# Matmuls of the identity in PE's planned pauses, and a new set of due times, in a four-layer graph attention kernel

## The chip, the cores and the metric

The kernel runs on one core of one Trainium2 chip. A core has five engines with instruction queues of their own: PE (TensorE, matmuls into PSUM), DVE (VectorE), ACT (ScalarE), POOL (GpSimd) and SP (SyncE, which only issues DMAs here). [...] The metric is the device time of one execution in microseconds (us); lower is better.

## What is computed

Sixteen graphs of 1024 nodes with 256 features each share one adjacency matrix (about 0.8% of the entries set, with the diagonal). Four layers follow one another. Each normalises, applies an attention over the neighbours, and adds the result to x:

```python
h = jnp.maximum(_layernorm(x, axis=-1), 0.0)
x = x + _L0_gnn_ref(h, adj, L0_gnn_W, L0_gnn_a)
...
x = x + _L1_gnn_ref(h, adj, L1_gnn_W, L1_gnn_a)
...
x = x + _L2_gnn_ref(h, adj, L2_gnn_W1, L2_gnn_W2, L2_gnn_W3)
...
x = x + _L3_gnn_ref(h, adj, L3_gnn_W, L3_gnn_a)
```

Layers 0 and 3 have four heads of 64 features. Their score for nodes i and j is `leaky_relu(s_src[i] + s_dst[j])`, masked by the adjacency, followed by a softmax over j and a product with the projected values. Layer 1 is the same with one head of 256. Layer 2's score is the product of two projections of h, and it ends in a relu where the others end in an elu. All is float32.

## The kernel before

The program has two paths. `fast` does the work; `general` is taken only when a check of the inputs fails, and is not run here.

`fast` doesn't issue instructions as it goes. It describes each piece of work as a step of a `Plan`: the engine that does it, a planned duration in us (`cost`), a due time, a function that will issue the instructions, the steps it comes after, and the buffers that it takes and gives back (`plan.add`, line 137 on). When all steps are described, `Plan.order` plays them through on paper: whenever an engine is idle, it starts, of the steps that are ready and whose buffers are free, the one with the earliest due time. A step's end is passed on to other engines 0.2 us later (`LATENCY`). The order in which the steps start in this play is the order in which their functions are then called, and so the order of the instructions in each engine's queue. The due times are priorities, not times at which anything is held back. On the chip each engine works through its queue in order and waits at semaphores, whatever the plan thought of the durations.

The due times come from tables. A period is 165.625 us (`PERIOD`). `LATER` shifts each (graph, layer), `AHEAD` and `LEAD` say how much earlier its opening part (`prologue`) is due, `STEP` spreads that part, `WHEN` places the weights and products of layers 1 and 2, and `SLOT` and `SLOT_LATER` place the sparse work. In `SLOT`, `gather` is how much earlier a gather is due than its unit, `load` is about the loading of x, and `again` and `once` about a second loading of x before the closing addition (of layers 3 and 0, line 1606), all in periods.

The work on PE is, with its planned cost:

- The projection of 128 nodes (`projected`, 0.9 us), from a transposed h that a DMA transpose makes (`move`, line 1311: 1.23 us on SP, then 1.6 and 0.9 us until it has landed), between two ACT copies.
- Layer 1 and 2: for each graph and layer eight steps `attend` (line 1854, 3.48 us), each a sum of eight products over 128 source nodes into one of two PSUM banks, `accb`. When it is done, DVE takes a reciprocal of column 256 (line 1871), and ACT divides columns 0 to 255 by it (line 1877 for layer 1, 1879 for layer 2), after which the bank is given back. Layer 2 has scores and queries on PE too (1.72 us each).
- Layers 0 and 3 of most graphs: sparse, in 15 slots of two (graph, layer) each. For 24 units of each slot, four gathers on POOL (`gather`, line 1735, planned at 1.31 us each) bring rows of a table through an indirect DMA into a `vg` tile, DVE weighs them (lines 1752 and 1761), and PE adds them up (line 1779, 0.94 us a unit). A `vg` tile, of which there are three, is free when PE is done with it.
- Layer 0 of the first graph and layer 3 of the last: dense, 64 steps each of 0.47 us (`steps_a`).

Nearly all matmuls are issued by the helper `product` (line 671, so the profile has them under line 674): one call with 128 stationary columns makes two matmuls of 64 columns each. [...] `buf` (line 666) asks for a tile anew each time that a step takes one, in the home that `Plan.homes` has worked out.

Of the kernel before, what the change touches and what calls it, by code (L numbers as in the profile page):

```python
# [21 lines left out]
P = 128  # L22
# [40 lines left out]
EDGED = {member: members for members in SLOTS for member in members}  # L63
BASE = [SLOT_AT[EDGED[b, 0]] if (b, 0) in EDGED else -0.6 for b in range(16)]
SLOT = {
    'span': 0.6715, 'at': 0.002, 'gather': 0.1559, 'begin': 6.8964, 'load': -2.6706, 'close': 0.8376,
    'edges': 30.2125, 'fill': -5.4149, 'weigh': -0.8387, 'attend': 0.309, 'rows': 0.0278, 'again': -1.2003,
    'once': 0.9411, 'pace': 9.064,
}
SLOT_LATER = {  # L70
    ((1, 0), (2, 0)): 0.1347, ((3, 0), (0, 3)): 0.7221, ((4, 0), (5, 0)): 1.2356, ((6, 0), (1, 3)): 0.946,
    ((7, 0), (2, 3)): 0.8656, ((8, 0), (3, 3)): 1.3324, ((9, 0), (4, 3)): 0.7329, ((10, 0), (5, 3)): 0.8829,
    ((11, 0), (6, 3)): 0.574, ((12, 0), (7, 3)): 0.5056, ((13, 0), (8, 3)): 0.8959, ((14, 0), (9, 3)): 0.7223,
    ((15, 0), (10, 3)): 0.6366, ((11, 3), (12, 3)): 0.9472, ((13, 3), (14, 3)): 1.4115,
}

PERIOD, EARLY = 165.625, 0.983  # L80
START = {0: 0.0, 1: 1.0154, 2: 2.027, 3: 3.1446}
LEAD = {0: 1.3047, 1: 0.0738, 2: 0.8011, 3: -0.2537}
STEP = {0: 0.0638, 1: 0.019, 2: 0.0837, 3: 0}
WHEN = {
    (1, 'weights'): ((0.3988, 0.0481), (1.6881, 0.9484)),
    (1, 'attended'): ((-0.0661, 0.0535), (0.5757, 0.1965)),
    (2, 'weights'): ((0.0014, 0.0211), (0.2452, 0.0602)),
    (2, 'attended'): ((0.4029, 0.0849), (0.4921, 0.1455)),
}

LATER = {
    (0, 0): 0.6744, (0, 1): 0.7927, (0, 2): 0.8401, (0, 3): 0.6401, (1, 0): -0.0906, (1, 1): 0.6495,
    (1, 2): 0.7052, (1, 3): -0.2464, (2, 0): 0.3847, (2, 1): 0.9636, (2, 2): 1.6293, (2, 3): 0.9684,
    (3, 0): 0.2871, (3, 1): 1.8347, (3, 2): 0.909, (3, 3): 1.7204, (4, 0): 0.2668, (4, 1): 0.9127,
    (4, 2): 0.5106, (4, 3): 0.7991, (5, 0): 0.4493, (5, 1): 1.167, (5, 2): 1.8896, (5, 3): 1.2478,
    (6, 0): 1.4069, (6, 1): 1.2537, (6, 2): 1.2951, (6, 3): 1.3435, (7, 0): 1.6461, (7, 1): 1.1917,
    (7, 2): 0.9305, (7, 3): 2.4128, (8, 0): 1.1808, (8, 1): 0.8157, (8, 2): 1.1351, (8, 3): 1.4491,
    (9, 0): 0.2849, (9, 1): 0.6946, (9, 2): 1.0782, (9, 3): 0.8714, (10, 0): 0.848, (10, 1): 1.0053,
    (10, 2): 1.2988, (10, 3): 1.4282, (11, 0): -0.0568, (11, 1): 0.5794, (11, 2): 1.0036, (11, 3): 0.5035,
    (12, 0): 1.2348, (12, 1): 0.8426, (12, 2): 0.8101, (12, 3): 0.8823, (13, 0): 0.5907, (13, 1): 0.6373,  # L100
    (13, 2): 1.2291, (13, 3): 2.0887, (14, 0): 1.1378, (14, 1): 0.1377, (14, 2): 0.8184, (14, 3): 3.6396,
    (15, 0): 0.4651, (15, 1): 1.0589, (15, 2): 2.2223, (15, 3): 5.4015,
}
AHEAD = {
    (0, 0): 5.3604, (0, 1): -3.9636, (0, 2): 1.0958, (0, 3): 0.4878, (1, 0): 4.4827, (1, 1): 1.3166,
    (1, 2): 1.1058, (1, 3): -3.1414, (2, 0): 1.5105, (2, 1): 0.7138, (2, 2): 0.588, (2, 3): 0.6503,
    (3, 0): -0.0881, (3, 1): 2.6718, (3, 2): 2.0939, (3, 3): 0.3548, (4, 0): -0.0676, (4, 1): 0.1131,
    (4, 2): -0.1087, (4, 3): -1.4402, (5, 0): 1.0665, (5, 1): -0.4301, (5, 2): 0.6188, (5, 3): 0.6455,
    (6, 0): -0.8488, (6, 1): 0.3608, (6, 2): 3.0352, (6, 3): 0.3675, (7, 0): -0.3494, (7, 1): -0.2156,
    (7, 2): 1.5593, (7, 3): 1.6384, (8, 0): -0.2572, (8, 1): 2.3309, (8, 2): 0.0821, (8, 3): 0.5845,  # L110
    (9, 0): -1.7754, (9, 1): -0.1769, (9, 2): 2.3775, (9, 3): -0.289, (10, 0): 0.5044, (10, 1): 0.0591,
    (10, 2): -0.0652, (10, 3): 0.1443, (11, 0): -4.6604, (11, 1): -0.1943, (11, 2): 0.7395, (11, 3): -0.9007,
    (12, 0): 0.5393, (12, 1): 0.2581, (12, 2): 3.9858, (12, 3): -2.992, (13, 0): 0.2891, (13, 1): -0.1296,
    (13, 2): 0.2842, (13, 3): -0.9502, (14, 0): 0.2928, (14, 1): -0.0225, (14, 2): 0.1627, (14, 3): 8.5761,
    (15, 0): 0.4367, (15, 1): -1.2495, (15, 2): 2.7098, (15, 3): 0.9033,
}


# [3 lines left out]
class Plan:  # L122
# [5 lines left out]

    LATENCY = 0.2
    TURN, PATIENCE = 0.12, 3.0  # L130

    def __init__(self, free, strict):
        self.free, self.steps, self.wide = dict(free), [], set()
# [16 lines left out]
    def order(self):  # L150
# [9 lines left out]
        for k, s in enumerate(steps):  # L160
            if not left[k]:
                ready[s[0]].append((s[2], k))
        events, now, res, last_wide = [], 0.0, [], False
        self.starts, self.turns = {}, []

        def fits(k):
# [8 lines left out]
        while True:  # L175
            again = True
            while again:
                again = False
                for engine, queue in ready.items():
                    if not idle[engine] or not queue:  # L180
                        continue
                    queue.sort()
                    pick = next((q for q in queue if fits(q[1])), None)
                    if pick is None:
                        continue
                    cost = steps[pick[1]][1]
                    if engine == PE:
                        wide = pick[1] in self.wide
                        if wide != last_wide:
                            stay = (  # L190
                                q for q in queue
                                if q[0] < pick[0] + self.PATIENCE and (q[1] in self.wide) == last_wide and fits(q[1])
                            )
                            pick = next(stay, pick)
                        turns = (pick[1] in self.wide) != last_wide
                        cost = steps[pick[1]][1] + self.TURN * turns
                        last_wide ^= turns
                    queue.remove(pick)
                    k = pick[1]
                    self.turns.append((k, True))  # L200
                    for tag in steps[k][5]:
                        free[tag] -= 1
                    for tag in set(steps[k][5]) & set(at):
                        at[tag] += 1
                    idle[engine] = engine == LAND
                    res.append(k)
                    self.starts[k] = now
                    again = True
                    heapq.heappush(events, (now + cost, k, 0))
                    heapq.heappush(events, (now + cost + self.LATENCY, k, 1))  # L210
            if not events:
                break
            now, k, what = heapq.heappop(events)
            if what == 0:
                idle[steps[k][0]] = True
            else:
                self.turns.append((k, False))
                for tag in steps[k][6]:
                    free[tag] += 1
            for b in behind[k]:  # L220
                if (steps[b][0] == steps[k][0]) == (what == 0):
                    left[b] -= 1
                    if not left[b]:
                        ready[steps[b][0]].append((steps[b][2], b))
# [406 lines left out]
def fast(  # L631
# [34 lines left out]
    def buf(tag, shape, dtype=F32, name=None):  # L666
        pool = psum if tag in ("pp", "acc", "accb") else sb
        home = plan.at[plan.now, tag].pop(0)[1]
        return pool.tile(shape, dtype, name=name or tag, tag=f"{tag}_{home}", bufs=1)

    def product(to, stationary, moving, start, stop):

# [1045 lines left out]
    def steps_c(slot):  # L1718
# [8 lines left out]
        for u in range(UNITS):  # L1727
            t, kt = divmod(u, TILES)
            at = slot.at + SLOT["span"] * PERIOD * u / UNITS
            for g in range(NG):  # L1730

                def gather(u=u, g=g):
                    if g == 0:
                        T["vg", u] = buf("vg", [P, NG, slot.width])
                    nc.gpsimd.indirect_dma_start(  # L1735
                        out=T["vg", u][:, g, :],
                        out_offset=None,
                        in_=slot.table[:, :],
                        in_offset=bass.IndirectOffsetOnAxis(ap=edge_of[:, u * NG + g : u * NG + g + 1], axis=0),
                        bounds_check=N - 1,  # L1740
                        oob_is_err=False,
                    )

                s = plan.add(
                    POOL, 1.31, at - SLOT["gather"] * PERIOD, gather, (*slot.stored, *edges_ready) if g == 0 else (s,), take=() if g else ("vg",)
                )
            got = landed(s, at, 0.4 * slot.width)

# [47 lines left out]
    def steps_b(lay, dues):  # L1796
# [53 lines left out]
        for it in range(NT):  # L1850
# [1 line left out]
            at = dues("attended", it)  # L1852

            def attend(it=it, half=half, t=t):
                acc = T["acc", it] = buf("accb", [P, HALF])
                for jt in range(NT):
                    product(
                        acc[:, : F + 1],
# [240 lines left out]
```

## Time and profile before

| | |
|---|---|
| median of three runs | 3209.26 us |
| lowest and highest of them | 3188.41 and 3211.73 us |
| the profiled execution, its own time | 3179.46 us |
| its span, first to last instruction | 3177.7 us |
| mean granted PE clock | 0.941 |
| PE, DVE, ACT, POOL busy | 2703.7, 2321.0, 2113.2, 1757.8 us |
| `attend` of layers 1 and 2 (`accb`) | 8192 matmuls, 1004.1 us busy |
| gathers (line 1735) | 1440, mean 1122 ns |

The profiled execution is one of its own, 30 us below the median of the runs. The busy time of an engine is the union of its instructions' durations. The granted clock says how much of PE's full clock a throttle let through, as a mean over the stretch. A row of idle time or waits names the instruction whose semaphore came last.

### The profile page before, as it was taken

Reading aid. Unit: us, or ns where it says so; the run is one execution under the profiler, and the core shown is the slowest. Engines: PE = TensorE matmul, PEld = TensorE weight load, DVE = VectorE, ACT = ScalarE, POOL = GpSimd, SP = SyncE. Lnnn points to the kernel's source line nnn. Section 1 sums busy time; section 2 is a strip of 40 time slices with the busy share of each in tenths; the row PEclk is TensorE's granted clock in tenths of the full one; section 3 lists DMA queues with packets and bytes.
Section 4 is the critical chain, followed back from the end, with each engine's and each line's share of the span. In section 5 each row is a group of like instructions: output and inputs, shape, how many; then the busy total and the mean of one; then the engine's idle time right before and its main releaser. Section 6 shows DMA issues by size and latency. Waiting matters only on the chain. (4 is left out here: it accounts for less than half of the span.)

```text
span 3177.7 us, 65299 instructions
## 1 busy us (share of the span) xinstructions
PE 2703.7 (85%) x23759; PEld 1400.6 (44%) x23759; DVE 2321.0 (73%) x4581; ACT 2113.2 (67%) x5987; POOL 1757.8 (55%) x1570
## 2 busy tenths in 40 slices
PE   6577889788789899887989898999898899898787
PEld 4342454334446444343444444444444444344335
DVE  8786747777776677767767787878777776776578
ACT  5657695766868657777667767758676657567432
POOL 1046426765652456646656676666656654674570
PEclk9889899898899999999989999999999999999899
DMA  6346455756664467676665767667656654666551
GB/s 188 101 114 172 121 133 153 194 165 183 149 169 96 133 168 184 172 156 188 154 173 150 192 167 176 166 179 173 176 148 165 164 139 130 158 178 151 138 155 32
DMA packets 506519, 492.76 MB, mean 155 GB/s; under 512 B 317380, under 2 KB 428740, under 8 KB 506192
## 3 DMA queue, kind: packets, MB, share of 16 engines
q0 software_dynamic: 115200, 287.05, 33.1%
q1 hardware_dynamic: 390304, 200.67, 26.4%
q8 instruction: 192, 3.15, 0.4%
q14 instruction: 135, 1.11, 0.1%
q10 hardware_dynamic: 688, 0.79, 0.1%
HBM read 460.65 MB, written 65.01 MB: 165 GB/s over the span
## 5 line engine op out<-in xcount | busy, mean ns | idle before, releaser
L1735 POOL DMA_INDIRECT vg<-table,edge_of x1440 | 1615.8, 1122 | 1024.2 <-PE acc L1779 478.1
L674 PE MATMUL accb<-val,p 128*64 128x257 f32 x8192 | 1004.1, 390 | 70.2 <-issue 34.7
L1761 DVE TENSOR_TENSOR vg<-vg,w 128x1040 f32<-128x1040 f32 x720 | 895.0, 1243 | 26.0 <-issue 0.2
L674 PEld LDWEIGHTS accb<-val,p 128*64 128x64 f32 x8192 | 618.9, 140 | 442.3 <-issue 137.6
L1779 PE MATMUL acc<-vg,pick 128*32 128x260 f32 x5760 | 472.9, 405 | 95.3 <-DVE vg L1761 51.4
L674 PE MATMUL pp<-w,hTp 128*64 128x264 f32 (+1 forms) x3072 | 426.9, 412 | 113.5 <-ACT hTp L1325 45.6
L674 PE MATMUL pp<-qT,hT 128*64 128x512 f32 x2048 | 482.0, 604 | 19.4 <-issue 6.8
L674 PEld LDWEIGHTS pp<-w,hTp 128*64 128x64 f32 x3072 | 225.5, 144 | 303.9 <-issue 103.8
L1779 PEld LDWEIGHTS acc<-vg,pick 128*32 128x32 f32 x5760 | 173.7, 112 | 402.1 <-issue 164.5
L1281 ACT ACTIVATE h<-xt,nshift,rstd 128x256 f32<-128x256 f32 x512 | 276.2, 597 | 59.7 <-DVE nshift L1243 41.9
L1307 ACT COPY planes<-h 128x512 uint16<-128x512 uint16 x496 | 281.8, 621 | 20.5 <-DMA turned<-planes 18.3
L1599 ACT ACTIVATE o<-acc,rden 128x64 f32<-128x64 f32 x960 | 219.2, 323 | 101.0 <-DVE rden L1592 66.7
L674 PEld LDWEIGHTS pp<-qT,hT 128*64 128x64 f32 x2048 | 147.6, 138 | 283.7 <-issue 235.1
L1836 ACT ACTIVATE u<-pp 128x512 f32<-128x512 f32 x256 | 154.8, 605 | 152.6 <-PE pp L674 84.8
L1240 POOL TENSOR_TENSOR rstd<-rstd,neg_half 128x8 f32<-128x8 f32 (+2 forms) x67 | 122.6, 1831 | 221.0 <-DVE rstd L1237 186.0
L1325 ACT COPY hTp<-turned 128x1024 uint16<-128x1024 uint16 x184 | 213.4, 1168 | 24.1 <-DMA turned<-planes 20.3
L1380 ACT ACTIVATE vs<-pp,vs 128x64 f32<-128x64 f32 x960 | 223.3, 316 | 0.0
L1193 DVE BATCH_NORM_STATS2 bn<-xt 128x6 f32<-128x256 f32 x512 | 203.2, 421 | 17.9 <-DMA xt<-in_x_dram 4.4
L1841 DVE SCALAR_TENSOR_TENSOR p<-u,p 128x512 f32<-128x512 f32 x256 | 175.3, 685 | 46.0 <-ACT p L1837 34.1
L674 PE MATMUL pp<-w2v,hT 128*64 128x256 f32 x1024 | 154.8, 437 | 63.0 <-ACT hT L1325 45.6
L1564 DVE SCALAR_TENSOR_TENSOR o<-ex,o 128x512 f32<-128x512 f32 (+1 forms) x256 | 142.0, 555 | 69.9 <-ACT ex L1560 58.1
L1842 DVE TENSOR_TENSOR p<-p,mask 128x512 f32<-128x512 f32 x256 | 177.1, 692 | 8.8
(153 smaller groups left out, 2440.7 us busy)
## 6 DMA issues: line engine op xcount, KB each, us to landing
table<-vs SPq DMA_DIRECT2D x120, 264.0 KB
xt<-in_x_dram SPq DMA_DIRECT2D x123, 256.0 KB
vg<-table,edge_of POOLq DMA_INDIRECT x1440
out_dram<-xt SPq DMA_DIRECT2D x64, 256.0 KB
kept<-xt SPq DMA_DIRECT2D x60, 256.0 KB
xt<-kept SPq DMA_DIRECT2D x60, 256.0 KB
raw<-in_adj_dram SPq DMA_DIRECT2D x32, 256.0 KB
row<-er_d SPq DMA_DIRECT2D x32, 256.0 KB
```

The costliest lines, as they stand in the source:

```text
L674: nc.tensor.matmul(to[c : c + COLS], stationary[:, c : c + COLS], moving, start=start, stop=stop, skip_group_check=True,)
L1193: nc.vector.bn_stats(mean_var[b][:, t, :, :].rearrange("p s e -> p (s e)"), of[b, t // 2][:, t % 2, :])
L1281: nc.scalar.activation(h, (x_in if layer == 0 else x_tiles)[b, t // 2][:, t % 2, :], AF.Relu, bias=T["shift"][:, t : t + 1], scale=T["rstd ...
L1307: nc.scalar.copy(to[:, :, :, k, :], of)
L1325: nc.scalar.copy(bits, T["tp", t0].rearrange("p s c q -> p c q s"))
L1380: nc.scalar.mul(to[:, hd, :], of[:, hd, :], a[:, hd, :])
L1599: nc.scalar.mul(to[:, hd, :], of[:, hd, :d], rden[:, hd, :])
L1735: nc.gpsimd.indirect_dma_start(out=T["vg", u][:, g, :], out_offset=None, in_=slot.table[:, :], in_offset=bass.IndirectOffsetOnAxis(ap=edge ...
L1761: nc.vector.tensor_tensor(values, values, w[:, :, m, :].unsqueeze(3).to_broadcast([P, NG, heads, d + 1]), OP.mult)
L1779: nc.tensor.matmul(acc[g * GROUP : (g + 1) * GROUP], pick[:, u, g * GROUP : (g + 1) * GROUP], vg[:, g, lo : lo + heads * (d + 1)], start=k ...
L1841: nc.vector.scalar_tensor_tensor(p, u, 1.0, p, op0=OP.max, op1=OP.mult)
L1842: nc.vector.tensor_mul(p, p, mask_of(half, jt))
```

## The change

Three things are changed.

First, `Plan.order` notes when PE was busy. Whenever PE is idle in the play and no step can start, it adds up PE's planned busy time in the last 3.4 us. If that is under 65% and PE has steps left, it puts in a step of 0.45 us that takes no buffer and comes after nothing, at that place of the order. PE is then taken for 0.45 us in the play too. The step's function, `keep_busy`, issues two products of the identity with itself, 128 columns each, into columns 384 to 511 of the first `accb` bank. Their result is never read.

Second, the two `accb` tiles are made once, before all steps, and `attend` picks one of them by the home that the plan worked out. Before, each `attend` asked for a new tile in that home.

Third, all tables of due times have other values, and the planned cost of a gather is 1.45 us where it was 1.31. The mean of `LATER`'s 64 entries goes from 1.07 to 0.39 periods, that of `SLOT_LATER`'s 15 from 0.84 to 0.18, that of `AHEAD`'s 64 from 0.51 to 0.62.

```diff
 SLOT = {
-    'span': 0.6715, 'at': 0.002, 'gather': 0.1559, 'begin': 6.8964, 'load': -2.6706, 'close': 0.8376,
-    'edges': 30.2125, 'fill': -5.4149, 'weigh': -0.8387, 'attend': 0.309, 'rows': 0.0278, 'again': -1.2003,
-    'once': 0.9411, 'pace': 9.064,
+    'span': 0.6625, 'at': 0.0375, 'gather': 0.0743, 'begin': 6.4905, 'load': -1.9066, 'close': 0.7661,
+    'edges': 31.0052, 'fill': -2.7808, 'weigh': -0.8326, 'attend': 0.4626, 'rows': 0.0277, 'again': 0.9994,
+    'once': 0.595, 'pace': 9.064,
 }
...
-PERIOD, EARLY = 165.625, 0.983
-START = {0: 0.0, 1: 1.0154, 2: 2.027, 3: 3.1446}
-LEAD = {0: 1.3047, 1: 0.0738, 2: 0.8011, 3: -0.2537}
-STEP = {0: 0.0638, 1: 0.019, 2: 0.0837, 3: 0}
+PERIOD, EARLY = 165.625, 1.0283
+START = {0: 0.0, 1: 1.0294, 2: 2.0269, 3: 3.1395}
+LEAD = {0: 1.2991, 1: 0.0803, 2: 1.0096, 3: -0.2434}
+STEP = {0: 0.0519, 1: 0.0021, 2: 0.137, 3: 0.0046}
...
 LATER = {
-    (0, 0): 0.6744, (0, 1): 0.7927, (0, 2): 0.8401, (0, 3): 0.6401, (1, 0): -0.0906, (1, 1): 0.6495,
...
+    (0, 0): -2.2609, (0, 1): 0.3716, (0, 2): -0.1125, (0, 3): -0.5687, (1, 0): -2.2721, (1, 1): -0.4437,
...
     TURN, PATIENCE = 0.12, 3.0
+    SPAN, SHARE, FILL = 3.4, 0.65, 0.45
+    fill = None
...
         events, now, res, last_wide = [], 0.0, [], False
+        stretches, pe_left = [], sum(s[0] == PE for s in steps)
...
                     idle[engine] = engine == LAND
+                    if engine == PE:
+                        stretches.append((now, now + cost))
+                        pe_left -= 1
...
             if not events:
                 break
+            if self.fill and idle[PE] and pe_left:
+                share, n = 0.0, len(stretches) - 1
+                while n >= 0 and stretches[n][1] > now - self.SPAN:
+                    share += stretches[n][1] - max(stretches[n][0], now - self.SPAN)
+                    n -= 1
+                if share < self.SHARE * self.SPAN:
+                    k = len(steps)
+                    steps.append([PE, self.FILL, now, self.fill, (), (), ()])
+                    behind.append([])
+                    stretches.append((now, now + self.FILL))
+                    idle[PE] = False
+                    res.append(k)
+                    self.starts[k] = now
+                    heapq.heappush(events, (now + self.FILL, k, 0))
             now, k, what = heapq.heappop(events)
...
+    banks = [psum.tile([P, HALF], F32, name=f"bank{n}", tag=f"bank{n}", bufs=1) for n in range(bufs["accb"])]
+
+    def keep_busy():
+        for n in range(2):
+            product(banks[0][:, HALF - P :], ident, ident, True, True)
+
+    plan.fill = keep_busy
...
-                    POOL, 1.31, at - SLOT["gather"] * PERIOD, gather, (*slot.stored, *edges_ready) if g == 0 else (s,), take=() if g else ("vg",)
+                    POOL, 1.45, at - SLOT["gather"] * PERIOD, gather, (*slot.stored, *edges_ready) if g == 0 else (s,), take=() if g else ("vg",)
...
-                acc = T["acc", it] = buf("accb", [P, HALF])
+                acc = T["acc", it] = banks[plan.at[plan.now, "accb"].pop(0)[1]]
```

## The prediction

> **What bounds the kernel now.** I read the page first: busy shares, the forty slices with the granted clock, and the chain of waits.
>
> ```profile
> span 3177.7 us, 65299 instructions
> ...
> PE 2703.7 (85%) x23759; PEld 1400.6 (44%) x23759; DVE 2321.0 (73%) x4581; ACT 2113.2 (67%) x5987; POOL 1757.8 (55%) x1570
> ...
> PEclk9889899898899999999989999999999999999899
> ...
> PE 19%; DVE 10%; issue 4%; DMA 3%; ACT 3%; another core or an unknown queue 2%; POOL 1%; POOLq 0%; DVEq 0%; SPq 0%; ACTq 0%
> ```
>
> PE is the fullest engine, but 474 us of the span find it idle. The chain's shares add up to 42%: it was followed back only that far. Of what was followed, PE is 19/42 = 0.45, and DVE 0.24. So I reckon that one us put on PE, or taken off it, moves the end by 0.45 us.
>
> Then the core's clock (mean 0.941) and one place where it fell, cut into windows of 3.41 us; columns are the window's length, busy time of each engine (instructions), clock, DMA share and GB/s.
>
> ```profile
> 1373.57:1376.99 3.42, 3.09 (x32) 1.79 (x31) 2.79 (x6) 3.31 (x10) 2.94 (x4) 1.00 1.17 298
> 1376.99:1380.40 3.41, 0.00 (x0) 0.00 (x0) 3.35 (x10) 0.00 (x0) 2.77 (x4) 1.00 1.24 118
> 1380.40:1383.81 3.41, 0.00 (x0) 0.00 (x0) 1.84 (x5) 0.41 (x1) 2.92 (x3) 0.50 1.10 119
> 1383.81:1387.23 3.42, 1.60 (x8) 1.00 (x10) 2.29 (x2) 1.76 (x9) 0.66 (x1) 0.50 1.08 133
> 1387.23:1390.64 3.41, 3.41 (x18) 1.86 (x18) 0.44 (x2) 1.48 (x3) 0.00 (x0) 0.50 0.82 234
> 1390.64:1394.05 3.41, 3.41 (x36) 2.16 (x34) 3.34 (x5) 3.41 (x18) 0.00 (x0) 1.00 0.10 35
> ```
>
> A window without matmuls is followed by half the clock; a full window brings it back. All clock changes of the trace lie on this one grid. What half the clock costs shows in two pieces of the timeline, the same eight projection matmuls at half and at full clock:
>
> ```profile
> 1385.63 2.03 PE L674 MATMUL pp<-w,hTp 128*64 128x264 f32 x8 [8.97 <-ACT vs L1380]
> ...
> 2023.61 1.09 PE L674 MATMUL pp<-w,hTp 128*64 128x264 f32 x8
> ```
>
> Last, waits (engine and line, what ended the wait, total us, times, longest), and pieces of the chain (start, us):
>
> ```profile
> POOL vg L1735 <- issue: 357.4, 1160, 2.1
> ...
> DVE w L1752 <- DMA vg<-table,edge_of: 137.1, 70, 6.5
> ...
> PE accb L674 <- ACT o L1879: 19.6, 8, 4.6
> ```
>
> ```profile
> 1935.47 9.68 DMA turned<-planes
> ...
> 1965.52 9.31 DMA turned<-planes
> ```
>
> A gather takes 1.12 us, and 0.30 us of issue lies before most; the plan reckons 1.31. A DMA transpose is planned at 1.23 + 1.6 + 0.9 = 3.73 us and cost the chain over 9 here. So the plan is early in places.
>
> **Part one: the clock.** Counted from the trace's clock records, half clock holds in 61 stretches, 376 us together; PE is busy for 264 us of them. At full clock that work takes half: 132 us of PE at most, times 0.45 = 59 us. [...] In the trace 59 of 813 full-clock windows are followed by half clock, and only 11 of the 59 were nearly empty (busy under 5%): every window busy under 40% was followed by it (45), of those from 40 to 60% 14 in 53, above 60% none in 715. [...] Returning asks more: no half-clock window busy under 75% brought the full clock back.
>
> How much goes? Fills stand where the plan pauses. A pause from a late transfer, like the 9 us above, isn't planned, or is planned short. I take half of the half-clock time: 66 us of PE, −30 us. The ends are 0 and −59.
>
> **Part two: the fills.** One fill is two products, each of two column halves. The trace has 8192 instructions for 256 `attend` steps of 16 calls, so a float32 call is two instructions: 8 in a fill, 128 columns each. An `attend` of 32 instructions takes 3.48 us in the chain, 109 ns each for 257 columns; by columns a fill is 8 x 109 x 128/257 = 0.43 us, beside the plan's 0.45. How many: the rule (PE idle, under 65% of the last 3.4 us busy) laid over the trace's own pauses gives 453, in 158 pauses. The planned work is less than the traced: 256 x 3.48 + 320 x 1.72 + 512 x 0.9 + 360 x 0.94 + 128 x 0.47 + 90 x 0.9 = 2380 us. If the plan is as long as the run it pauses for some 800 us, not 474: up to 760 fills. I take 600, 270 us, for 4,800 matmuls and as many weight loads. Where PE would wait anyway they cost nothing: that cover is the 474 us. Where the plan's pause isn't there, because PE is late, the next real step waits for them. If all were so: 270 x 0.45 = 122 us; none: 0. I take 15%: 40 us of PE, +18 us. PEld at 44% isn't limiting. Keeping both `accb` tiles for the whole program instead of asking anew adds no instruction: 0, since each bank is still reused in the same PE order.
>
> **Part three: a new wait.** A fill writes columns 384 to 511 of `banks[0]`, the bank that half of the `attend` steps use. DVE's reciprocal and ACT's division read it. [...] By addresses the fill (columns from 384) and the readers (up to 256) need no wait and this part costs 0; by bank, every fill queued after a pending read waits for it, and all of PE behind it; DVE and ACT reads queued after a fill wait for the fill, 0.45 us. No row of before has two such users of one bank. The nearest is PE's wait for the reader before it reuses a bank: 19.6 us for line 1879 and 11.1 for line 1877. From above: read ends lie a median 5.2 us (mean 8.8) after the `attend`; at 63 of the 158 pauses a read of one of the two alternating banks is pending, and at 53 it outlasts the pause, by 367 us together. That would be 165 us on the end. It happens only where the read stands ahead of the fill in the planned order, and then PE's next step often waits for the same lagging ACT. I take the near row, 31 us: +14 us.
>
> **Part four: the order.** All due times change, so every engine's and queue's order does, SP's loads and stores, POOL's gathers and the DMA waits behind them. No row prices an order; its bounds are those of waits that it can move. In the followed part the chain waits for gathers (1.8% of the span, 57 us), transposes (1.5%, 48) and an unknown queue (1.6%, 51): 156 us, and I let this go either way. What can be read: a gather now costs 1.45 in the plan, near 1.12 + 0.30 = 1.42; before, 1440 of them were planned 158 us too short, so the planned work on them came too early. Reloads of x for layer 3 get `again` 0.9994 for −1.2003, that is 2.2 periods of 165.6 us earlier against their use. Both give waits for transfers more room. The price is a load holding its `xr` tile longer. Of 156 I take about a third: −50 us.
>
> Sum: −30 + 18 + 14 − 50 = −48 us on the profiled execution's 3179.5, 3131. That execution lies 30 us under the median of the runs; against the median 3209 it is **3161 us**, and I say 3160.
>
> **The rivals.** *PE tied to ACT (slower).* The bank wait is the rule and not the exception. For it: the 5.2 us lag. Against: only 31 us of waiting for the same readers now. At 60% of 367 us it is 220 us of PE, 99 us on the end: 3179.5 − 30 + 18 + 99 − 50 = 3217, by the median 3246. It decides from 46% on: 31 + 48/0.45 = 138 us eats the gain, and 209 us (57%) is 1% slower. *Fills in front of ready work.* Pauses lie elsewhere than planned: half of the fills on ready work, +61, clock gain only 10: 3179.5 − 10 + 61 + 14 − 50 = 3195, by the median 3224, no change that can be told. For it: unplanned lateness. Against: the plan has more pauses than the chip. *It doesn't do what it says.* The cold windows are the late transfers', the clock stays at 0.94 to 0.95, and the order gives ±30: 3180 to 3240.
>
> **How the numbers follow.** A measurement here can tell 1%, 32 us. The forecast faster by over that: 0.42; the two cases about nothing: 0.27; slower, by the bank wait or an order that collides with late transfers: 0.31. The forecast's own range is 3090 to 3177 (order −120 and the clock's full 59 at one end). For 8 in 10 the range runs to the slower case's 3246 and some way beyond, as its waits are bounded only by 165 us: 3095 to 3265.
>
> **What would show it.** Right: mean clock at 0.965 or more, 4,000 to 6,000 matmuls of identity on line 674, under 60 us of waits of theirs for lines 1871, 1877 and 1879, less waiting for gathers. Wrong: fills with idle time before them ended by ACT's `o` or DVE's `rden`; the clock unchanged with PE busier; or waits for transfers grown with the clock warm, then the order failed.

## The result, and the profile after

The changed kernel's median is 3195.88 us in 11 runs, that of the kernel before, run beside it, 3190.62 in 11. The ratio is 1.0031, with a 95% interval from 1.0009 to 1.0053: 0.3% slower, less than the 1% that the prediction counts as a change, and not the 1.5% faster that was forecast. The profiled execution took 3208.5 us, the longest of the 11.

The page of the changed kernel, with the lines that answer to those shown of before:

```profile
span 3206.8 us, 72484 instructions
...
PE 2865.2 (89%) x27351; PEld 1590.8 (50%) x27351; DVE 2322.6 (72%) x4581; ACT 2117.4 (66%) x5987; POOL 1767.3 (55%) x1570
...
PEclk9999999998999999999899999999999999999999
...
PE 57%; DVE 17%; ACT 9%; issue 8%; DMA 4%; another core or an unknown queue 3%; POOL 1%; SPq 0%; DVEq 0%; POOLq 0%; ACTq 0%
```

The clock did what the change is named for: its mean is 0.967 where it was 0.941, and by the clock records half clock holds for 215 us instead of 376. PE is 161.5 us busier all the same. This time the chain could be followed through almost the whole span, and PE is 57% of it.

Groups of PE's instructions (busy us, mean ns, then idle time before them and what ended it), and waits, of the changed kernel:

```profile
L703 PE MATMUL bank<-ident 128*64 128x128 f32 x3592 | 259.2, 283 | 35.0 <-issue 28.3 <-ACT o L1908 2.5 <-POOL ident masks.py:199 1.4
```

```profile
POOL vg L1764 <- issue: 352.6, 1146, 2.0
...
DVE w L1781 <- DMA vg<-table,edge_of: 72.5, 39, 6.6
...
PE bank L703 <- issue: 62.8, 138, 2.5
...
PE pp L703 <- issue: 34.8, 48, 3.9
...
PE acc L1808 <- issue: 17.2, 32, 1.9
PE pp L1500 <- issue: 17.1, 19, 2.6
...
PE bank L703 <- ACT o L1908: 14.3, 10, 3.4
```

PE's pauses without a wait in the kernel before:

```profile
PE pp L674 <- issue: 42.4, 50, 3.7
...
PE accb L674 <- issue: 34.7, 68, 1.0
...
PE acc L1779 <- issue: 33.6, 53, 6.1
...
PE pp L1471 <- issue: 14.6, 16, 3.5
```

There are 3592 / 8 = 449 fills. They wait 2.5 us in all for ACT, so the shared bank costs next to nothing. The wait for gathers fell from 137.1 to 72.5 us. In the new order without fills (e1 below) it is 79.6, in the old order with fills (e5) 107.7, so the new order has the larger part in this; whether by the 1.45 or by the other tables was not separated. Idle time of PE that ended with no wait at all ("issue") is 132.7 us in 239 pauses over all groups, against 125.2 us in 187 before. Of the 132.7, 28.3 us stand in front of fills.

### The profile page after: what moved, and what is told of

Same layout as the page of the kernel before. It is cut to its first block, busy times and chain, and to the rows that moved or that the text cites. A ratio compares the mean times of both kernels' runs of the same rounds, so it can differ in the third digit from the quotient of the medians.

```text
span 3206.8 us, 72484 instructions
## 1 busy us (share of the span) xinstructions
PE 2865.2 (89%) x27351; PEld 1590.8 (50%) x27351; DVE 2322.6 (72%) x4581; ACT 2117.4 (66%) x5987; POOL 1767.3 (55%) x1570
## 4 chain that ended last, share of the span: by engine, by line
PE 57%; DVE 17%; ACT 9%; issue 8%; DMA 4%; another core or an unknown queue 3%; POOL 1%; SPq 0%; DVEq 0%; POOLq 0%; ACTq 0%
PE pp L703 24%; PE bank L703 22%; PE acc L1808 9%; DVE vg L1790 6%; DMA vg<-table,edge_of 2%; DVE p L1674 1%; ACT h L1310 1%; DVE p L1837 1%; DVE bn L1222 1%; DMA turned<-planes 1%; ACT hTp L1354 1%; DVE xt L1595 1%; ACT planes L1336 1%; ACT vs L1409 1%
## 5 line engine op out<-in xcount | busy, mean ns | idle before, releaser
L703 PE MATMUL bank<-val,p 128*64 128x257 f32 x8192 | 992.2, 387 | 51.9 <-issue 34.5
L703 PEld LDWEIGHTS bank<-val,p 128*64 128x64 f32 x8192 | 618.9, 138 | 401.6 <-issue 126.3
L703 PE MATMUL pp<-w,hTp 128*64 128x264 f32 (+1 forms) x3072 | 418.8, 404 | 88.5 <-ACT hTp L1354 23.4
L1808 PE MATMUL acc<-vg,pick 128*32 128x260 f32 x5760 | 445.3, 397 | 51.9 <-DVE vg L1790 27.8
L703 PE MATMUL bank<-ident 128*64 128x128 f32 x3592 | 259.2, 283 | 35.0 <-issue 28.3
L703 PEld LDWEIGHTS bank<-ident 128*64 128x64 f32 x3592 | 213.4, 141 | 92.2 <-issue 76.9
L1593 DVE SCALAR_TENSOR_TENSOR o<-ex,o 128x256 f32<-128x256 f32 (+1 forms) x256 | 142.3, 556 | 86.7 <-ACT ex L1589 61.4
```

What stands on the lines that cost most here:

```text
L703: nc.tensor.matmul(to[c : c + COLS], stationary[:, c : c + COLS], moving, start=start, stop=stop, skip_group_check=True,)
L1808: nc.tensor.matmul(acc[g * GROUP : (g + 1) * GROUP], pick[:, u, g * GROUP : (g + 1) * GROUP], vg[:, g, lo : lo + heads * (d + 1)], start=k ...
```

## The experiments

The experiments ran on five chips, and all times are given as ratios to the kernel before on the same chip; the clock is that of the profiled execution. On the first three its median is 3218, 3190 and 3187 us. On the last two it is 2943 and 2949, 8% less; what is different there is shown below.

### No fills, old tables, tables alone, half a fill

Each is the changed kernel with one edit.

```diff
e1_no_products
-    plan.fill = keep_busy
+    plan.fill = lambda: None
e3_tables_only
-    plan.fill = keep_busy
e4_half_fill
-        for n in range(2):
+        for n in range(1):
             product(banks[0][:, HALF - P :], ident, ident, True, True)
```

e2_old_tables has the tables and the 1.31 of the kernel before, and the fills. In e1 the plan still has the fills, so every other instruction keeps its place.

> The order of the changed kernel, but its fills issue no matmuls. Theory A (the fills warm the clock and take the saving back by standing before ready work, about even): within 0.5% of the changed kernel, that is 0.998 to 1.008 of the kernel before, clock back to 0.94 to 0.95. Rival B (the fills earn the 1% that was forecast, and the new order loses it): 1.010 to 1.020 of before. Rival C (the fills cost more than they bring): 0.985 to 0.995 of before.

Measured: 0.9944 (0.9922 to 0.9965), clock 0.936.

> The fills with the due times and the gather cost of the kernel before. Theory A: 0.995 to 1.008 of before, clock about 0.965. Rival B: 0.980 to 0.992. Rival C: 1.010 or more.

Measured: 1.0973 (1.0927 to 1.1019).

> The new due times and gather cost, no fill in the plan either, so the order is planned without the pauses being taken. Theory A: 0.998 to 1.010 of before with a clock of 0.94. Rival B: 1.010 or more. Rival C: 0.985 to 0.995.

Measured: 1.0234 (1.0179 to 1.0288).

> The order of the changed kernel with one product in a fill instead of two (about 1800 matmuls instead of 3592). Theory A: 0.998 to 1.006 of before, clock between 0.945 and 0.965. Rival B: 1.005 to 1.012, between the changed kernel and the one whose fills issue nothing. Rival C: below the changed kernel's 1.003, about 0.997.

Measured: 1.0005 (0.9981 to 1.0030), clock 0.946.

Without its fills the new order is 0.6% faster than the kernel before; with half of each, even; with all, 0.3% slower. So here a colder clock was the better bargain. e2 and e3 say less than was hoped. The new tables are 2% slower than the kernel before when the plan has no fills, and the old tables 10% slower when it has them. By its number e3 lies in rival B's range and e2 in rival C's, but both only show that a table suits one plan, which the theories had left out.

Since e1 has the same PE instructions in the same order, but for the fills, the two traces can be laid beside one another matmul by matmul. For each real matmul I took the time since the one before it:

```
us between starts of real matmuls             without fills   with fills   difference
the 157 places where fills stand                      262.9        374.1       +111.3
other places with a pause                             377.8        347.0        -30.8
no pause, half clock without, full with fills         170.1         95.5        -74.6
no pause, full clock without, half with fills          31.9         56.6        +24.6
no pause, clock the same in both                     2324.1       2312.7        -11.4
sum                                                                             +19.1
```

A pause is idle time of PE over 0.15 us. One more place, the 158th, stands before the first matmul. A fill that no pause and no half clock breaks takes 0.446 us in the mean in the changed kernel's trace, start to start; so all would take 449 x 0.446 = 200 us. As traced they take 256 us, counted at each place from the first fill's start to the last one's and 0.1 us more, with half clock and unexplained pauses among them. At the 157 places PE pauses 210 us in e1, but not where the plan has the pauses: at 66 places e1 pauses under 0.2 us. Of the 256 us, 110 reach beyond the pause that e1 has at that place, and that is the growth of these places. Against it, the matmuls without a pause got 61 us shorter, and the other pauses 31.

These two executions were not run side by side: the one is the longest of its 11, the other is 10 us under its median, and the kernel before has 3191 us beside the one and 3218 beside the other. e7 and e6 below, the same order with three fills and with all, ran on one chip and say the same: the fills' places +117 us (111 of them beyond the pauses), matmuls without a pause -58, other pauses -30, sum +29.

### The fills alone in the old order; another bank; fewer; half the instructions

For e5 the plan of the kernel before is played with its own tables (the `accb` tiles are made once here too), and a fill is put into the order without making PE busy in the play, so the order of all other instructions is that of before. The cuts show in part what differs from the changed kernel:

```diff
e5_fills_in_old_order
-                    idle[PE] = False
                     res.append(k)
                     self.starts[k] = now
-                    heapq.heappush(events, (now + self.FILL, k, 0))
+                    filled = now + self.FILL
+                    heapq.heappush(events, (filled, k, 2))
e6_older_bank
-            product(banks[0][:, HALF - P :], ident, ident, True, True)
+            product(banks[1 - recent[0]][:, HALF - P :], ident, ident, True, True)
e7_fills_under_35
-                    steps.append([PE, self.FILL, now, self.fill, (), (), ()])
+                    fn = self.fill if share < 0.35 * self.SPAN else lambda: None
+                    steps.append([PE, self.FILL, now, fn, (), (), ()])
e8_half_the_instructions
-            product(banks[0][:, HALF - P :], ident, ident, True, True)
+            nc.tensor.matmul(
+                banks[0][:, HALF - 2 * (P - 1) :].rearrange("p (a b) -> p a b", a=2),
+                ident,
+                ident[:, : P - 1].unsqueeze(1).to_broadcast([P, 2, P - 1]),
+                start=True,
+                stop=True,
+                skip_group_check=True,
+            )
```

> The kernel before with its order untouched on every engine; fills by the same rule are issued in the pauses of its plan, but the plan doesn't see them. Theory D (a fill costs PE more than the pause hides, since many planned pauses aren't there on the chip, and the work that the warmer clock shortens is followed by waits that take the gain): 1.004 to 1.015 of before although the clock rises to 0.96 or more. Rival E (the fills help by themselves and only the new order wastes it): 0.980 to 0.993.

Measured: 1.0036 (1.0012 to 1.0060), clock 0.960. The fills cost 0.4% in an order that was not touched, with the clock warmer. So the loss doesn't need the new order.

> The changed kernel, but each fill writes into the accb bank that the last attend step did not use, whose readers are mostly done. If the shared bank ties PE and its readers (rival F): 0.993 to 0.998 of before. Theory D: no change from the changed kernel's 1.003, so 1.000 to 1.006.

Measured: 1.0034 (1.0010 to 1.0059), the changed kernel's own ratio. The bank is of no weight.

> The order of the changed kernel; a planned fill issues its matmuls only where PE's share of the last 3.4 us is under 35% instead of 65%. Theory D: fewer fills cost less, 0.994 to 1.000 of before, with a clock of 0.945 to 0.96. Rival E: like the changed kernel or slower, 1.002 to 1.008, since the clock is lost.

Measured: 0.9929 (0.9896 to 0.9961), clock 0.933. The edit kept three fills of 449, since the planned fills themselves hold the share over 35%. So it is a second run without fills, beside e6 on one chip: 1.0034 / 0.9929 = 1.011, the fills cost 1%.

> The changed kernel with the same PE time in a fill but half the instructions: two calls of 128 stationary columns and 254 moving ones instead of four of 64 and 128. If the idle time that no wait explains comes from fetching the fills' instructions (rival G, 30 us more of it than without fills): 0.996 to 1.000 of before. Theory D without it: 1.001 to 1.006.

Measured: 1.0028 (1.0006 to 1.0049), clock 0.980. The expectation had PE's time wrong: in this trace the instructions of 128 stationary columns start 214 ns apart, where in the changed kernel's fills two of 64 start within 109 ns (7 and 102 by turns), so a fill took 0.86 us, twice as long. Half the instructions with twice the time cost as much as before. By itself this separates nothing.

### One wide call, and fills by real pauses

e9 makes a fill of one such call: two instructions, 0.43 us. e10 keeps of the 449 fills those 284 that fit into pauses which PE had at the same place in the traces of e1 and e7; over the fills' places the pauses of the two runs correlate at 0.96, so most of a pause comes from the order. e11 keeps the other 165. The list of kept fills is in the code (`PAUSED`):

```diff
e9_one_wide_call
-        for n in range(2):
-            product(banks[0][:, HALF - P :], ident, ident, True, True)
+        nc.tensor.matmul(
...
e10_fills_in_real_pauses
     def keep_busy():
+        if next(fills) not in PAUSED:
+            return
e11_fills_elsewhere
     def keep_busy():
+        if next(fills) in PAUSED:
+            return
```

> The changed kernel; a fill is one call of 128 stationary columns by 254 moving ones, two instructions where it had eight, for about the same 0.43 us of PE. Rival G (what a fill costs beyond its time is the issuing of its instructions): 0.990 to 0.998 of before, with the clock still at 0.96. Theory D (its time in front of ready work): 1.001 to 1.006.

Measured: 0.9926 (0.9907 to 0.9945), clock 0.965.

> The order of the changed kernel; of its 449 fills 284 are kept, those that fit into pauses which PE had at the same place in both profiles of this order without fills (in 0.45 us steps of the shorter of the two pauses). Theory D (fills cost where the pause isn't there; the warm clock earns): faster than without fills (0.9944, 0.9929), so 0.980 to 0.991, clock 0.96. Rival H (the warmer clock brings the end nothing): 0.992 to 0.998, no better than no fills at all.

Measured: 0.9950 (0.9928 to 0.9973), clock 0.965.

> The complement: only the other 165 fills, which stand where PE had no pause or one too short for them. Theory D: slower than without fills by their 0.45 us each times PE's share of the chain, 74 us times 0.5: 1.003 to 1.008 of before, clock 0.94. Rival H (fills cost through something else, as much in real pauses): 0.995 to 1.000.

Measured: 0.9991 (0.9968 to 1.0013), clock 0.941.

e10 is where the idea should have paid: the clock as warm as in the changed kernel's profile, hardly a fill in front of ready work. It is not measurably faster than the order without fills (0.9944 and 0.9929), but these ran on other chips, and by the intervals 0.3% either way would not be seen. e11, with fewer fills and a colder clock, is 0.4% above e10 on the same chip: fills elsewhere cost. In the matmul-by-matmul comparison of e10 with e1 matmuls without a pause took 50 us less, and the fills' places 33 us more, 27 of them fill time beyond the pause.

e9 is as fast as no fills, with all 449 in place. Its fills in the profile:

```profile
L695 PE MATMUL bank<-ident 128*128 128x254 f32 x898 | 243.7, 408 | 9.5 <-issue 4.0 <-ACT o L1914 2.4 <-POOL ident masks.py:199 1.4
```

Unexplained pauses before fills are 4.0 us here and 28.3 in the changed kernel, and counted as above the fills take 198 us instead of 256, of which 68 reach beyond e1's pauses instead of 110. With fewer instructions in a fill fewer of these pauses fell among them. That spoke for the instructions of a fill as a part of its price.

### On two other chips

e12 is e1 once more. e13 is e10 with the wide call. e14 is e9 with three tiny calls (64 stationary columns by 4) behind the wide one. e15 is e5 with the wide call.

```diff
e14_wide_plus_small
+        for n in range(3):
+            nc.tensor.matmul(
+                banks[0][:COLS, HALF - 4 :], ident[:, :COLS], ident[:, :4], start=True, stop=True, skip_group_check=True
+            )
```

> The order of the changed kernel without fills, as the base for the others on this chip: 0.991 to 0.996 of before by every theory, clock 0.935.

Measured: 1.0095 (1.0067 to 1.0122), where it had been 0.9944.

> The 284 fills that fit real pauses, each one wide call of two instructions. If the warm clock earns what the matmuls gain times PE's share of the chain (some 50 us times 0.5): 0.8% below the run without fills, 0.983 to 0.989 of before. Rival H (it earns nothing at the end): equal to it within 0.3%, 0.990 to 0.997.

Measured: 1.0059 (1.0038 to 1.0080), clock 0.971: 0.4% below e12 (by the two intervals uncertain by about 0.3%), between the two expectations.

> All 449 fills, each the wide call of 0.43 us and three tiny calls of 64 by 4, so eight instructions again. Theory G (the issuing of the instructions costs): back at 1.000 to 1.006 of before. Theory D (PE time in front of ready work): like the one wide call, 0.991 to 0.996, at most 0.3% more for the tiny calls' own time.

Measured: 1.0393 (1.0368 to 1.0418), clock 0.991. No theory had this. In its trace, where calls of 128 and of 64 stationary columns follow one another, the step after each of a wide call's two instructions is 0.31 to 0.32 us instead of 0.21. PE is 97% busy. So more than the number of instructions differs from e9, and it is inconclusive for what it was made for.

> The kernel before with its own order, fills in its planned pauses, each one wide call. Theory G: the cost of 0.4% that the eight instructions had goes, 0.994 to 1.000 of before. Theory D: 1.002 to 1.006 as before.

Measured: 0.9975 (0.9957 to 0.9994), clock 0.985: the only version that beat the kernel before on such a chip. It wasn't tried on one of the others.

The last three are e1, e9 and the changed kernel once more, on the fifth chip.

> The order of the changed kernel without fills, beside the next two. On a chip whose traces show PE stalls that no wait explains: 0.991 to 0.996 of before. On a chip without them: 1.006 to 1.012.

Measured: 1.0091 (1.0060 to 1.0122), clock 0.948.

> All 449 fills, one wide call each. Theory G (the instructions of a fill are what costs, the warm clock earns little): within 0.4% of the run without fills, on the lower side. If PE time in front of ready work costs as well: 0.5% or more above it.

Measured: 1.0071 (1.0040 to 1.0101), clock 0.974.

> The changed kernel itself. Theory G: on a chip with the stalls 0.7 to 1.2% above the run without fills; on a chip without them less, 0 to 0.5%. If the cost has nothing to do with the stalls, about 0.9% above it on either.

Measured: 1.0041 (1.0014 to 1.0067), clock 0.975. On this chip the fills as they are earn 0.5% (1.0041 / 1.0091 = 0.9950, by the two intervals uncertain by about 0.4%), where they cost 1% on the other kind. The wide call, e17, earns 0.2%, by its interval no different from this. The sign of the order's effect turned too.

What differs is visible in PE's timeline. The same stretch, first in the changed kernel's first profile and then in e18's (start, us, instruction, idle time before it):

```profile
1424.64 1.08 PE L703 MATMUL pp<-w2v,hT 128*64 128x256 f32 x8
1425.56 0.61 PE L703 MATMUL bank<-ident 128*64 128x128 f32 x8
1425.99 3.64 PE L703 MATMUL bank<-val,p 128*64 128x257 f32 x31
1429.84 0.38 PE L703 MATMUL bank<-val,p 128*64 128x257 f32 x1 [0.20 <-issue]
1429.86 0.43 PE L703 MATMUL pp<-w2v,hT 128*64 128x256 f32 x1
1431.25 0.45 PE L703 MATMUL pp<-w2v,hT 128*64 128x256 f32 x2 [0.97 <-issue]
1431.99 0.38 PE L703 MATMUL pp<-w2v,hT 128*64 128x256 f32 x1 [0.28 <-issue]
1432.70 0.66 PE L703 MATMUL pp<-w2v,hT 128*64 128x256 f32 x4 [0.33 <-issue]
1433.29 1.08 PE L1808 MATMUL acc<-vg,pick 128*32 128x260 f32 x16
```

```profile
1336.69 1.08 PE L703 MATMUL pp<-w2v,hT 128*64 128x256 f32 x8
1337.61 0.61 PE L703 MATMUL bank<-ident 128*64 128x128 f32 x8
1338.04 3.65 PE L703 MATMUL bank<-val,p 128*64 128x257 f32 x32
1341.52 1.03 PE L703 MATMUL pp<-w2v,hT 128*64 128x256 f32 x8
1342.48 1.08 PE L1808 MATMUL acc<-vg,pick 128*32 128x260 f32 x16
```

Eight matmuls that take 1.03 us in the one take 3.4 us (1429.86 to 1433.29) in the other, one or two at a time, with pauses that no semaphore ends. Such a place is called a stall below. The profile of the kernel before has the 187 such pauses counted above, 125.2 us; taking those within 5 us of one another together, they stand at 80 places. Each trace of the first three chips has them, at 63 to 106 places, never quite the same. The traces of the other two chips have at most one, of 0.33 us or less. Inside a place they are regular: in the kernel before, 76 of the 107 steps from one pause's end to the next, up to 5 us, are 0.65 to 0.8 or 1.35 to 1.5 us long. DVE and ACT show them as waits for an unknown queue: 200 and 125 us in the profile before; the waits listed for e16 and e18 have none. Groups of the same matmuls without fills, in e1 and then in e16:

```profile
L703 PE MATMUL bank<-val,p 128*64 128x257 f32 x8192 | 999.6, 392 | 67.9 <-issue 36.0 <-ACT o L1908 20.1 <-ACT o L1906 5.7
L1808 PE MATMUL acc<-vg,pick 128*32 128x260 f32 x5760 | 474.5, 407 | 118.4 <-DVE vg L1790 65.9 <-issue 24.5 <-ACT o L1628 19.2
```

```profile
L703 PE MATMUL bank<-val,p 128*64 128x257 f32 x8192 | 949.7, 386 | 34.9 <-ACT o L1908 25.8 <-ACT o L1906 6.5 <-ACT planes L1336 1.2
L1808 PE MATMUL acc<-vg,pick 128*32 128x260 f32 x5760 | 458.7, 404 | 117.3 <-DVE vg L1790 102.1 <-ACT o L1628 14.3 <-PE acc L1808 0.6
```

"issue" is gone from the second, and the waits that the plan knows about are what is left. That these pauses make up most of the difference between chips shows matmul by matmul: the changed kernel's first trace and e18's have the same instructions, between their first and last matmul the first takes 231 us longer, and 190 of these lie at such pauses or within 1.5 us of one. Slower transfers don't show in the first: a DMA packet took 145 ns in it and 149 in e18's in the mean on queue q0, 34.7 and 35.5 on q1. The chain of e18:

```profile
PE 45%; DVE 19%; DMA 15%; ACT 10%; issue 7%; POOL 4%; SPq 0%; DVEq 0%; POOLq 0%; ACTq 0%
```

## Why the prediction was wrong

*The order, part four.* It was put at −50 us, by the waits that the order might move. Measured without fills (e1 and e7, with the banks made once) it is −0.56 and −0.71%, or −18 and −23 us, on the chips with the stalls, and +0.9%, +27 us, on those without. What it argued for came: the gather wait fell by 65 us. What failed is the step from that wait to the end. On the chip of e13 and e15 the new order waits less for gathers too (e13 first, then e15 with the old order), and it is the slower one:

```profile
DVE w L1801 <- DMA vg<-table,edge_of: 184.5, 102, 11.5
...
DVE w L1788 <- DMA vg<-table,edge_of: 253.2, 135, 8.6
```

Why the new order does better only where PE is stopped by pauses without a wait isn't shown.

*The fills, parts one to three.* Their sum was −30 + 18 + 14 = +2 us; measured on the chips with stalls it is 1.0031 − 0.9944, or +28 us, and on one chip (e6 and e7) 1.1%, or +33. Term by term:

- The fills' time. This is the term that failed. I took 600 fills with 15% on ready work, 40 us of PE; there were 449, and 110 us of their 256 reached beyond the pauses. The step behind it is that the 474 us of PE's idle time cover the fills. At the fills' places PE idles 210 us, and at 66 of them hardly at all.
- The clock. Half-clock time fell by 161 us of the 188 forecast. In the matmul-by-matmul table PE got 61 us faster where 66 was taken. The direction and the size on PE were right.
- The bank. 14 us was taken, on the assumption that fills and readers of one bank wait for one another. No run shows a cost of that size: with the fills moved to the other bank the ratio is 1.0034 beside 1.0031, and they waited 2.5 us for ACT.

The prediction turns PE's time into the end's by 0.45. The pairs below test that rate: each run with fills beside the one of the same order and chip with none or nearly none, and the changed kernel beside e1. The columns are the change of matmuls without a pause, the fill time beyond the other run's pauses, their sum times 0.45, and the difference of the measured ratios in us, uncertain by some 10 to 13.

```
us                            matmuls   fills beyond   x 0.45   measured
changed kernel, e1                -61           +110      +22        +28
e6, e7                            -58           +111      +24        +33
e8, e7                           -100           +202      +46        +32
e4, e1                            -32            +41       +4        +20
e13, e12                          -36            +13      -10        -11
e14, e12                          -93           +286      +87        +88
e17, e16                          -49            +71      +10         -6
e18, e16                          -51            +76      +11        -15
```

On the chips with stalls the sign is right in all four, and so it is in e13 and e14. In e17 and e18, all fills on the fifth chip, which has no stalls, it is wrong, and there the rate fails. With the measured sizes the prediction's own sum for the chips with stalls is −27 (clock) + 50 (fills) + 1 (bank) − 18 (order) = +6 us, beside the 3195.88 − 3190.62 = +5 that was measured. That it comes so near is luck, as the terms are from single traces and several chips; which terms were mis-sized is not.

Of the rivals, the slower one (PE tied to ACT) is refuted by e6, and the one in which the clock stays cold by the clock of 0.967. What came is near the second, fills in front of ready work, which was put at 3224 us by the median of before, or +0.5%: its +61 us for the fills stands beside 50. But it left the order's gain at −50 and gave the clock only −10, and so was right for partly wrong reasons. Most signs of being right came too (clock 0.967, 2.5 us of waits of fills for ACT, less waiting for gathers; the fills' matmuls were 3592 and not 4,000 to 6,000), and the time did not follow: none of them measures the fill time beyond the pauses.

Two side sums of the prediction don't come out. 138 us are 38% of 367, not 46%; and an order of −120 with the clock's full 59 leads to 3062, not to 3090. The failure doesn't hang on either.

*What stays open.* Why the fills cost 1% on the one kind of chip and earn 0.5% on the other. A part is seen: the fills' places grow by 111 us in the changed kernel against e1 and by 81 in e18 against e16, and the 28 us of unexplained pauses before fills are missing in e18:

```profile
L703 PE MATMUL bank<-ident 128*64 128x128 f32 x3592 | 234.1, 281 | 5.9 <-ACT o L1908 3.4 <-POOL ident masks.py:199 1.4 <-ACT o L1906 0.4
```

Over all of PE, though, such pauses are hardly more with fills than without (132.7 us against 125.2 in e1), so the 30 us more that the expectation of e8 reckons with aren't there. e9 speaks for the number of instructions; e8 has 74.5 us of such pauses, 1.3 before fills, but its fills take twice the PE time and reach 202 us beyond the pauses of e7, and it was as slow. e9's base without fills was not run on its chip. What the stalls are isn't shown by any of these traces.

## What to carry to other kernels

Filler work takes PE's time where it outlasts the pause that it stands in. Here 110 us of it did, against 61 us by which the matmuls without a pause got shorter with the warmer clock. So price it by the pauses that a trace shows at those places of the order, not by the sum of all idle time and not by a plan's pauses, and by the time that the filler takes in the trace (256 us here), not by its time at full clock (200). A due-time table that suits one plan can be 2 to 10% slow in another (e2, e3), and a shorter wait for one transfer is no gain at the end by itself. A gain under 1% should be measured on more than one chip: here the sign of both halves of a change depended on it.

## What the runs showed of the hardware

- Five chips gave two times for the kernel before, 3187 to 3218 us on three and 2943 and 2949 on two. What was seen to differ in the traces is pauses of PE that no wait explains: 125 us of them in one trace of the kernel before, at most 0.33 us in any trace of the two faster chips. Of 231 us between two traces of the changed kernel, 190 lie at such pauses or within 1.5 us of one.
- In the changed kernel's trace too, all changes of the granted clock lie on one grid of 3.41 us. Of its full-clock windows the 27 with PE busy under 40% were all followed by half clock, of those from 40 to 60% 12 in 45, and of the 803 above 60% none.
- In a fill of the changed kernel the matmuls of 64 stationary columns by 128 start 7 and 102 ns apart by turns (medians at full clock). Instructions of 128 by 254 start 214 ns apart in e8; in e14, with calls of 64 stationary columns between them, the step after each is 0.31 to 0.32 us.
